# Moving the small Newton steps from GpSimd to VectorE in a fused scan and mixture-of-experts kernel, with a new order of the first loads and another way to sum two tiles of experts

## The chip, the cores and the metric

The kernel runs on one core of a Trainium2 chip. A core has five engines, each of which carries out its own instructions in the order in which they stand in its stream: TensorE (PE; its weight loads are listed apart as PEld), VectorE (DVE), ScalarE (ACT), GpSimd (POOL) and SyncE (SP). SP only issues DMA transfers here; POOL issues some too. The engines wait for each other by semaphores. PE writes into PSUM, the other memory is SBUF, and all tensors start and end in DRAM. The metric is the device time of one execution in microseconds (us).

## The reference, cut to what matters

The input `x` has 8 batches of 1024 rows of 256 values, in float32. One block of a network is computed: a layer norm with a shift and a scale per batch, a selective state-space scan, a residual, a second layer norm, a mixture of 8 experts of which each row takes the best two, and a second residual.

```python
h = _layernorm(x, axis=-1) * (1 + ca) + sa
x = x + ga * attn(h)
h = _layernorm(x, axis=-1) * (1 + cb) + sb
x = x + gb * ffn(h)
# attn: 16 states n for each of the 256 channels d
dt = softplus(dt_raw @ W_dt.T + b_dt);  A = -exp(A_log)
state[l] = exp(dt * A[n]) * state[l-1] + dt * h * B[n]     # a scan over the 1024 rows
y = sum_n state * C[n] + h * D
# ffn: probs = softmax(h @ Wg); the gates of the two best, summing to 1
out = sum over the two best e of gate[e] * (h @ We[e] + be[e])
```

The vectors `sa, ca, ga, sb, cb, gb` come from `silu(c) @ wmod`, one set per batch.

## The kernel before, in words

**Stages.** The rows are cut into 16 stages of 512 rows, two per batch; a stage has four tiles of 128 rows. Channels lie on the 128 partitions in two halves (`j` = 0, 1), so a tensor of one stage is 128x1024. Stages are numbered from 0 here; stage 14 is the last but one.

**The scan part** (`state`, L1001) runs over the 16 states `n`. For each, POOL makes `v` = `du` times the row of B that a DMA has spread over all partitions (L1029, one 128x1024 instruction), ACT makes `a` = exp(dt A) (L1040, two), and DVE scans (L1051, two). Then the scan's result is multiplied by the row of C: by DVE in two 128x512 instructions into `hcD` (L1065), or by POOL in one 128x1024 instruction in place in `hs` (L1070). Which of the two does it is written in `C_ENG`, a letter D or P for each `n`: one string for stages 0 and 1, one for the first halves of batches (stages 2, 4 ... 12), one for the second halves (3, 5 ... 13), one for stages 14 and 15. PE adds the 16 products up in PSUM while it transposes them (L1122). ACT keeps the last column for the next stage (L1057, L1061).

**The norms** (`statistics` L781, `factors` L799). DVE takes mean and variance of each tile (L786, L789); ACT makes a first guess of 1/sqrt(variance + eps) (L808 to L811); and one Newton step improves it, five instructions on 128x8 values, `newton` (L813), each of which needs the one before it. They are POOL's. The first norm of stage s+2 and the second norm of stage s share one Newton step, so there are 14 of this size (back parts of stages 0 to 13), two for the first norms of stages 0 and 1, one for stage 14 and two for stage 15.

**The experts** (`back`, L1149). The normed rows are split in a high and a low part; PE makes the logits; seventeen small instructions of DVE and ACT pick the two best ("route"). The gates go, as a high part by ACT (L1297) and a low part by POOL (`gates_lo`, L1299), through PE to the sum of the biases. For each tile and each pair of experts PE makes six matmuls into one PSUM bank (`expert_pair`, L1336). In stages 0 to 14 ACT weighs the two results by the gates (L1418), and PE adds them up by four transposing matmuls (L1428); a sum of two tiles is scaled by `gb` on ACT (L1435), turned back by PE (L1443), copied by ACT (L1449), and POOL's DMA adds it in DRAM to the `x` that SP has stored there (L1501). In stage 15 (`finish`, L1349) DVE adds each expert's result times its gate to an accumulator in SBUF (L1363), multiplies by `gb` (L1370), adds `x` (L1374), and SP stores the tile.

**What sets the order.** When the program is built, every operation is handed to a planner (`Plan`, L230) with an engine, an assumed cost, the data that it needs, the buffers that it takes, and a due time from the table `DUE` (L35), one number or one per phase (stage 0, stage 1, stages 2 to 13, stage 14, stage 15). `emit` (L304) plays the engines through in assumed time; whenever an engine is free it takes, among the operations that could start within that engine's `PATIENCE`, the one with the lowest due time. The order found so is written out as the fixed order of each engine's stream, DMA queues included. On the chip nothing is reordered: an instruction that waits holds up all behind it on its engine. The first loads are in `setup` (L518): on SP's queue c, wmod, x of stages 0 and 1, W_x, W_dt, be; on POOL's the four small ones D, A, Wg, b_dt. DVE also does the small setup work there (`clamp`, L642: four instructions on 128x16 values, twice).

Of the kernel before, what the change touches and what calls it, by code (L numbers as in the profile page):

```python
# [13 lines left out]
ALU = mybir.AluOpType  # L14
# [15 lines left out]
C_ENG = ("DDPDDPDDPDDPDDPD", "DPDDPDPDPDPDPDDD", "DPDPDPDPDPDPDPDD", "DDPDDPDDPDDPDDDD")  # L30
AHEAD = 1668.1
PATIENCE = {"ACT": 0.14, "DVE": 0.13, "PE": 0.25, "POOL": 0.5, "SP": 0.28}
# [5 lines left out]
    "load c": -2243.51,  # L38
    "load wmod0": -2004.07,
    "load wmod1": -1988.48,  # L40
    "load wmod2": -2.06,
    "load wmod3": -1957.81,
    "load W_x": -1.71,
    "load W_dt": -1965.24,
    "load b_dt": -116.61,
    "load A": -369.4,
    "load D": -1656.1,
    "load Wg": -357.62,
    "Wg hi": -1640.08,
    "Wg lo": -1616.04,  # L50
    "c^T": -414.35,
    "exp c": -1984.89,
    "1 + exp c": -351.35,
    "1 / c": -1644.2,
    "silu c": -1648.48,
    "mod1": -29.89,
    "mod1 out": -1640.92,
    "mod1 + 1": -57.77,
    "mod2": -97.07,
    "mod2 out": -2072.57,  # L60
    "mod3": -2117.64,
    "mod3 out": -1963.21,
    "mod3 + 1": -1953.8,
    "ga0": -437.02,
    "ga1": -460.54,
    "ga2": -73.86,
    "ga3": -2623.36,
    "gb0": -1953.35,
    "gb1": -357.52,
    "gb2": -461.1,  # L70
    "gb3": -27.31,
    "ga mod": -63.28,
    "ga mod D": 262.7,
    "1 / ga": -76.35,
    "gb^T": 279.89,
    "gb out": -406.31,
    "gb store": -483.98,
    "W_x^T": -3768.39,
    "W_x out": -436.84,
    "W_dt^T": -374.71,  # L80
    "W_dt out": -436.11,
    "exp A": -369.97,
    "-A": -74.32,
    "be rows": -2072.64,
    "be hi": -98.66,
    "be lo": -1963.34,
    "be": -55.72,
    "eps": -4332.43,
    "gates hi": (-235.79, -2460.72, -339.79, -149.99, -1797.16),
    "gates lo": (-24.1, -2044.84, -2133.06, -343.23, -3860.41),  # L90
    "load be": -15.49,
    "iw": -70.2,
    "load x": (-1989.96, -1978.86, -17.48, 8.4, -7.21),
    "stats1": (-2009.67, -1972.63, -69.27, -86.05, 47.99),
    "aggr1": (-1640.3, -1975.3, -1.3, -91.31, -2296.04),
    "before1": (-107.3, 986.06, -2961.9, -2961.25, -2977.69),
    "rstd1": (-359.36, 14.85, -2578.96, -2707.53, -2572.88),
    "norm1": (-24.76, -3800.78, 53.71, -15.89, -19.88),
    "trans1_0": (-2098.37, 28.07, -3664.64, -2478.96, -2711.13),
    "modg_0": (962.12, -427.57, -16.09, -2517.23, -444.87),  # L100
    "modD_0": (-1969.85, -43.93, -15.26, 0.47, -464.06),
    "trans1_1": (-2098.96, -16.51, -1646.42, -70.34, -17.88),
    "modg_1": (962.68, 28.65, -3869.23, -4.95, -390.32),
    "modD_1": (-16.02, -141.37, -3869.42, -2640.81, -526.1),
    "W_x / ga": (-2440.92, -1341.87, -50.77, -365.17, -1339.66),
    "proj": (-46.32, -3262.07, -1417.18, -7075.25, -1106.5),
    "rows": (-113.21, 892.07, -2147.14, -25.83, -373.01),
    "spill": (-1509.92, -46.65, -82.13, -108.28, -408.55),
    "dt0": (-2836.1, -86.93, -410.11, -472.19, -22.27),
    "softplus0": (8.96, -483.31, -563.94, -2696.95, -430.27),  # L110
    "dt1": (-2436.14, 985.9, -367.41, -1987.69, -75.38),
    "softplus1": (-3763.28, -2241.26, -2842.46, -2274.94, -367.03),
    "du": (-486.18, -2239.99, -70.63, -2154.13, -1629.08),
    "load B": (-1369.55, -17.6, -22.69, -296.42, -29.81),
    "load C": (-0.98, -16.67, 9.77, -2484.98, -15.04),
    "v": (-499.25, -85.1, -76.35, -47.8, 21.22),
    "a0": (-416.33, -341.56, -12.06, -392.16, -398.23),
    "a1": (-2633.56, -2630.9, -2268.36, -376.87, -2271.91),
    "scan0": (-345.29, -130, -84.13, -483.71, 835.51),
    "keep0": (-2622.16, -2801.29, -2480.02, -431.11, -2842.99),  # L120
    "C0": (-421.59, -408.48, -2258.73, -2296.35, -21.24),
    "scan1": (-350.22, -136.94, -86.02, -2760.06, -4.38),
    "keep1": (-2229.92, -335.27, -2547.2, -437.52, -439.8),
    "C1": (-414.5, -73.48, -2299.69, -2313.25, -19.25),
    "C": (-493.68, -127.22, -2167.24, -2223.87, 18.97),
    "y D": (19.24, -476.83, -54.5, -465.41, -8.25),
    "y": (-2254.19, -1637.88, -9.88, -1109.95, -3.56),
    "y C": (-473.82, -1635.95, -9.36, -7.82, 0.38),
    "load We": 4.3,
    "We hi": 992.95,  # L130
    "We lo": -499.19,
    "x + y": (-2642.38, -4495.38, -2303.57, -15.13, 893),
    "store x": (-2250.83, -2697.53, -2498.03, -14.55, -4714.94),
    "stats2": (-456.02, -1616.02, -2198.38, 0.86, -442.22),
    "aggr2": (-1761.59, -1623.66, -1485.56, 4.02, -32.11),
    "before2": (-53.78, -586.98, -7.88, 277.95, -2145.97),
    "rstd2": (-1659.97, -76.28, -71.01, -1965.28, -301.08),
    "norm2": (-15.76, -2440.99, -2156.75, 21.3, -62.97),
    "trans2_0": (-427.62, -2364.93, -1608.28, -17.84, 261.41),
    "hi0": (-2629.72, -4055.61, -4630.1, -3019.49, -2113.5),  # L140
    "mod2_0": (-343.91, -1615.01, -2238.87, -947.94, -35.03),
    "lo0": (-1317.6, -80.15, -2289.65, -464.16, 16.03),
    "trans2_1": (-3111.61, -1780.04, -10.03, -2604.76, 261.39),
    "hi1": (-2600.7, -738.55, -2256.02, 51.68, -2142.05),
    "mod2_1": (-359.16, -1823.24, -2242.34, -2256.16, 65.08),
    "lo1": (-2347.63, -3887.63, -77.67, -574.96, -1738.61),
    "logits^T": (-86.05, 0.71, -4.18, 0.12, 26.21),
    "logits out": (-2084.24, -89.2, -2470.09, -2118.52, -71.72),
    "logits": (-589.23, -70.63, -1938.4, -18.59, -408.58),
    "route": (-2625.88, -2360.01, -3907.92, -64.39, -2292.96),  # L150
    "gates": (-133.28, -75.36, -3858.04, -2448.11, -2203.07),
    "gates^T": (-2898.97, -1962.73, -2234.43, -4003.16, 6.19),
    "gates out": (-85.21, -9.58, -616.13, -18.22, -363.26),
    "biases": (-1642.72, -1.18, 6.14, 4.55, -932.33),
    "expert0": (-1632.13, -334.88, 2.48, 0.74, 28.86),
    "weigh0": (-2623.2, -2251.01, -2465.87, -2251.67, -3291.15),
    "sum0": (-1630.65, -2.35, 6.77, 2.59, 343.88),
    "gb": (-6.16, -2002.75, -2252.74, -1770.24, -2231.99),
    "turn": (13.97, 2.84, 5.77, -17.42, 288.49),
    "out": (-2240.75, -63.84, -406.3, -1777.56, -2456.12),  # L160
    "expert1": (-89.29, -20.09, 1.79, 275.85, 64.81),
    "weigh1": (-5.26, -122.87, -2272.08, -2165.17, -179.06),
    "sum1": (-5.22, -8.29, 3.93, 280.73, -101.5),
    "store": (-32.73, -46.88, -15.77, 11.83, -2124.92),
    "load gb": (-1904.24, -1904.24, -1904.24, -1904.24, -2839.22),
    "last bias": -92.62,
    "last": -2205.05,
    "last expert": 307.58,
    "last store": -16.76,
# [252 lines left out]
def kernel(  # L422
# [23 lines left out]
    nc = tc.nc  # L446
# [71 lines left out]
    def setup():  # L518
# [6 lines left out]
        def add(kind, eng, cost, fn, r=(), w=(), use=(), psm=None, xfer=0.0, duty=1.0, table=None):  # L525
            ring = [(rings[k], k) for k in use] + ([("psm", psm)] if psm else [])
            cold = 2.0 if duty == 1.0 else 1.3
            plan.add(
                kind, eng, cost, 0.0, fn, r=r, w=w, ring=ring, xfer=xfer, duty=duty, cold=cold, table=table
            )  # L530

        def load(kind, xfer, out_, in_, w, use=(), eng="SP"):
            q = nc.sync if eng == "SP" else nc.gpsimd
            add(
                kind, eng, 0.475 if eng == "SP" else 0.95, lambda: q.dma_start(out=out_(), in_=in_), w=[w],
                use=use, xfer=xfer,
            )
# [97 lines left out]
        add("mod1", "PE", 2.8, lambda: mod_mm(0, 2, pm), r=[sc_k, wm_k[0]], w=[pm], psm=pm, duty=0.05)  # L635
        add("mod1 out", "DVE", 0.15, lambda: mod_out(0, 2, pm), r=[pm], w=[m01])
        add("mod1 + 1", "DVE", 0.07, lambda: plus1(1), w=[m01])
        add("mod2", "PE", 1.4, lambda: mod_mm(2, 3, pg), r=[sc_k, wm_k[1]], w=[pg], psm=pg, duty=0.05)
        add("mod2 out", "DVE", 0.09, lambda: mod_out(2, 3, pg), r=[pg], w=[m2])

        ts, stt = nc.vector.tensor_scalar, nc.vector.scalar_tensor_tensor
# [921 lines left out]
```

## Time and profile before

| | us |
|---|---|
| median of 3 runs | 1039.54 (1039.06 to 1041.3) |
| the profiled execution, its own time | 1040.26 |
| its span, first to last instruction | 1038.5 |
| busy: DVE, PE, POOL, ACT | 959.8, 928.7, 918.5, 845.7 |
| first scan starts, last scan ends | 34.67, 988.66 |

The span is 1.8 us shorter than the execution's own time; the rest lies around it. Busy time counts an engine's instructions as they overlap in time; matmuls are pipelined, so a busy PE need not be at its peak. In a timeline line the columns are start, duration, engine, line of the kernel, operation, output and inputs with shapes and count, and in brackets the idle time before it and what ended that. In a group's line the numbers behind the bar are busy us, mean ns of one, and idle us before. In a table of windows each row has the stretch, its length, and the busy us of each engine with the number of instructions.

From the starts of the scans the stages can be told apart: the 32 scans of stage 2 begin at 154.9, those of stage 13 at 800.2, of stage 14 at 861.6, of stage 15 at 925.3. In between a stage takes 58.5 to 59.5 us from stage 5 to stage 12.

### The profile page before, as it was taken

Reading aid. Unit: us, or ns where it says so; the run is one execution under the profiler, and the core shown is the slowest. Engines: PE = TensorE matmul, PEld = TensorE weight load, DVE = VectorE, ACT = ScalarE, POOL = GpSimd, SP = SyncE. Lnnn points to the kernel's source line nnn. Section 1 sums busy time; section 2 is a strip of 40 time slices with the busy share of each in tenths; the row PEclk is TensorE's granted clock in tenths of the full one; section 3 lists DMA queues with packets and bytes.
Section 4 is the critical chain, followed back from the end, with each engine's and each line's share of the span. In section 5 each row is a group of like instructions: output and inputs, shape, how many; then the busy total and the mean of one; then the engine's idle time right before and its main releaser. Section 6 shows DMA issues by size and latency. Waiting matters only on the chain. (4 is left out here: it accounts for less than half of the span.)

```text
span 1038.5 us, 17114 instructions
## 1 busy us (share of the span) xinstructions
PE 928.7 (89%) x5525; PEld 739.9 (71%) x5525; DVE 959.8 (92%) x1488; ACT 845.7 (81%) x1845; POOL 918.5 (88%) x515
## 2 busy tenths in 40 slices
PE   6656798798899989999999989999998998999998
PEld 4444676586676868687777868688686867778886
DVE  3798999999999999999999999999999998999947
ACT  5855678889699988988899988988898986988661
POOL 4999879999999999999999999999999997988600
PEclk9657998899899999999999999999999999999999
DMA  6556327375655647475665737475575637656102
GB/s 203 185 182 219 122 88 234 96 209 147 194 157 156 208 108 211 113 217 155 166 221 146 219 85 212 123 209 175 138 240 128 221 67 204 169 148 198 39 6 46
DMA packets 103865, 165.20 MB, mean 159 GB/s; under 512 B 10160, under 2 KB 37216, under 8 KB 103776
## 3 DMA queue, kind: packets, MB, share of 16 engines
q1 hardware_dynamic: 95728, 156.22, 49.4%
q0 software_dynamic: 8048, 7.89, 5.1%
q8 instruction: 44, 0.72, 0.3%
q14 instruction: 45, 0.37, 0.1%
HBM read 146.76 MB, written 17.31 MB: 158 GB/s over the span
## 5 line engine op out<-in xcount | busy, mean ns | idle before, releaser
L1029 POOL TENSOR_TENSOR v<-du,bb 128x1024 f32<-128x1024 f32 x255 | 605.8, 2404 | 17.8 <-DMA bb<-bcd 11.7
L1040 ACT ACTIVATE a<-dt,negA 128x512 f32<-128x512 f32 x512 | 348.5, 697 | 52.9 <-DVE hcD L1065 33.0
L1070 POOL TENSOR_TENSOR hs<-hs,cc 128x1024 f32<-128x1024 f32 x96 | 229.9, 2396 | 17.1 <-issue 8.7
L1065 DVE TENSOR_TENSOR hcD<-a,cc 128x512 f32<-128x512 f32 x320 | 214.2, 684 | 13.9 <-ACT carry L1057 7.0
L1418 ACT ACTIVATE wt<-pe,G 128x256 f32<-128x256 f32 x480 | 201.6, 474 | 18.5 <-PE pe L1340 16.8
L1122 PE MATMUL y<-ident,hcD 128*128 128x128 f32 x1280 | 183.3, 285 | 34.8 <-DVE hcD L1065 34.6
L1051 DVE TENSOR_TENSOR_SCAN a<-a,v 128x512 f32<-128x512 f32 x166 | 195.6, 1213 | 8.5 <-POOL v L1029 4.8
L1051 DVE TENSOR_TENSOR_SCAN a<-a,carry,v 128x512 f32<-128x512 f32 x154 | 196.2, 1277 | 1.4 <-POOL v L1029 0.7
L1122 PEld LDWEIGHTS y<-ident,hcD 128*128 128x128 f32 x1280 | 153.8, 147 | 58.0 <-DVE hcD L1065 44.2
L1340 PE MATMUL pe<-we_hi,hi 128*128 128x512 f32 x512 | 179.2, 431 | 7.3 <-ACT wt L1418 4.3
L1340 PE MATMUL pe<-we_lo,hi 128*128 128x512 f32 x512 | 160.7, 395 | 0.0
L1340 PE MATMUL pe<-we_hi,lo 128*128 128x512 f32 x512 | 160.5, 395 | 0.0
L1428 PE MATMUL ma<-ident,wt 128*128 128x128 f32 x960 | 135.8, 275 | 1.2 <-ACT wt L1418 1.2
L1122 PE MATMUL y<-ident,hs 128*128 128x128 f32 x768 | 109.7, 285 | 24.2 <-POOL hs L1070 23.9
L1051 DVE TENSOR_TENSOR_SCAN hs<-a,carry,v 128x512 f32<-128x512 f32 x102 | 125.2, 1266 | 0.0
L1428 PEld LDWEIGHTS ma<-ident,wt 128*128 128x128 f32 x960 | 112.1, 141 | 16.2 <-ACT wt L1418 2.0
L1122 PEld LDWEIGHTS y<-ident,hs 128*128 128x128 f32 x768 | 92.1, 146 | 37.4 <-POOL hs L1070 31.1
L1340 PEld LDWEIGHTS pe<-we_lo,hi 128*128 128x128 f32 x512 | 96.3, 188 | 22.9
L1340 PEld LDWEIGHTS pe<-we_hi,lo 128*128 128x128 f32 x512 | 96.1, 188 | 23.1
L1051 DVE TENSOR_TENSOR_SCAN hs<-a,v 128x512 f32<-128x512 f32 x90 | 106.3, 1208 | 0.0
L1340 PEld LDWEIGHTS pe<-we_hi,hi 128*128 128x128 f32 x512 | 81.5, 190 | 25.6 <-ACT wt L1418 9.2
L831 ACT ACTIVATE xn<-x,ln 128x256 f32<-128x256 f32 x128 | 72.0, 599 | 3.0 <-POOL ln L820 3.0
(134 smaller groups left out, 936.9 us busy)
## 6 DMA issues: line engine op xcount, KB each, us to landing
bb<-bcd SPq DMA_DIRECT2D x256, 256.0 KB, 5.5
cc<-bcd SPq DMA_DIRECT2D x256, 256.0 KB, 5.2
x<-in_L_attn_u_dram SPq DMA_DIRECT2D x16, 512.0 KB, 3.7
out_dram<-x SPq DMA_DIRECT2D x15, 512.0 KB, 3.4
out_dram<-of POOLq DMA_DIRECT2D x15, 512.0 KB, 12.1
wf<-in_L_ffn_We_dram SPq DMA_DIRECT2D x8, 256.0 KB, 4.1
wm<-in_L_wmod_dram SPq DMA_DIRECT2D x2, 512.0 KB
bcd<-xd SPq DMA_DIRECT2D x32, 32.0 KB, 1.6
```

What stands on the lines that cost most here:

```text
L831: nc.scalar.activation(new("xn", xn, [P, TG, D])[:, k, :], T[x][:, k0 + k, :], AF.Identity, bias=T[ln][:, 1, o + k : o + k + 1], scale=T[l ...
L1029: nc.gpsimd.tensor_tensor(new("v", v, [P, DC, CL])[:, :, :cl], T["du", s][:, :, :cl], both(T[bb][:, :cl]), ALU.mult,)
L1040: nc.scalar.activation(new("a", a + (j,), [P, CL])[:, :cl], T["dt", s][:, j, :cl], AF.Exp, scale=negA[:, j, n : n + 1],)
L1051: nc.vector.tensor_tensor_scan(part(j), T[a + (j,)][:, :cl], T[v][:, j, :cl], init, ALU.mult, ALU.add)
L1065: nc.vector.tensor_tensor(new("hcD", hc, [P, DC, CL])[:, j, :cl], part(j), T[cc][:, :cl], ALU.mult)
L1070: nc.gpsimd.tensor_tensor(o, o, both(T[cc][:, :cl]), ALU.mult)
L1122: nc.tensor.matmul(new("y", y, [P, 2, D])[:, k % 2, j * P : (j + 1) * P], T[src][:, j, k * P : (k + 1) * P], ident, is_transpose=True, sta ...
L1340: nc.tensor.matmul(pe, T[v][:, j, k * P : (k + 1) * P], w[:, j, 2 * q : 2 * q + 2, :].rearrange("p e d -> p (e d)"), start=n == 0, stop=n ...
L1418: nc.scalar.activation(new("wt", wt, [P, 2, D])[:, i, :], T["pe", s, part, q, k][:, i * D : (i + 1) * D], AF.Copy, scale=T[G][:, k, e : e ...
L1428: nc.tensor.matmul(o[:, j, (k % 2) * P : (k % 2 + 1) * P], T["wt", s, q, k][:, i, j * P : (j + 1) * P], ident, is_transpose=True, start=Fa ...
```

## The change

Three things are named, and the whole plan is searched anew around them.

1. The Newton step's five instructions and the low part of the gates become VectorE's. The string of `C_ENG` for stages 2, 4 ... 12 goes from six P to seven.
2. The due times of the first loads change: on SP's queue x of stage 0 comes first, then be, c, wmod (first part), W_dt, x of stage 1, wmod (second and fourth part), We, W_x; on POOL's queue the order becomes b_dt, D, Wg, A, and the planner assumes that POOL's small loads share the DMA engines with less weight (`pkt` 0.02 in place of 0.1), so that it counts on their landing later.
3. In stage 14 the tiles 2 and 3 are treated like those of stage 15: bias, eight weighted additions per tile by DVE, times `gb`, plus `x`, and one store per tile by SP. The stores of `x` and POOL's adding store of that stage cover tiles 0 and 1 alone, and `gb` is loaded once, for stage 14.

Besides, all of `DUE` and some assumed costs are new (they change only the order), and three orderings within PE's own stream are written as dependencies.

```diff
-C_ENG = ("DDPDDPDDPDDPDDPD", "DPDDPDPDPDPDPDDD", "DPDPDPDPDPDPDPDD", "DDPDDPDDPDDPDDDD")
-AHEAD = 1668.1
-PATIENCE = {"ACT": 0.14, "DVE": 0.13, "PE": 0.25, "POOL": 0.5, "SP": 0.28}
+C_ENG = ("DDPDDPDDPDDPDDPD", "DPDPDPDPDPDPDPDD", "DPDPDPDPDPDPDPDD", "DDPDDPDDPDDPDDDD")
+AHEAD = 1833.68
+PATIENCE = {"ACT": 0.14, "DVE": 0.22, "PE": 0.23, "POOL": 0.51, "SP": 0.18}
...
-    "load x": (-1989.96, -1978.86, -17.48, 8.4, -7.21),
+    "load x": (-4389.52, -120.89, -66.7, 11.15, 0.38),
...
-    "load c": -2243.51,
-    "load wmod0": -2004.07,
+    "load c": -2337.1,
+    "load wmod0": -122.63,
...
-                kind, eng, 0.475 if eng == "SP" else 0.95, lambda: q.dma_start(out=out_(), in_=in_), w=[w],
-                use=use, xfer=xfer,
+                kind, eng, 0.475 if eng == "SP" else 0.8, lambda: q.dma_start(out=out_(), in_=in_), w=[w],
+                use=use, xfer=xfer, pkt=0.1 if eng == "SP" else 0.02,
...
-            r, m, v, tt = row(0), row(1), row(2), nc.gpsimd.tensor_tensor
+            r, m, v, tt = row(0), row(1), row(2), nc.vector.tensor_tensor
             tt(m, r, r, ALU.mult)
             tt(m, m, v, ALU.mult)
-            nc.gpsimd.tensor_scalar(m, m, -0.5, 1.5, ALU.mult, ALU.add)
+            nc.vector.tensor_scalar(m, m, -0.5, 1.5, ALU.mult, ALU.add)
             tt(r, r, m, ALU.mult)
             tt(m, row(3), r, ALU.mult)
...
-        plan.add("rstd" + n_, "POOL", 0.95 + 0.055 * n, t, newton, r=[st], w=[ln])
+        plan.add("rstd" + n_, "DVE", 0.4, t, newton, r=[st], w=[ln])
...
+        ts_ = tg if s < len(stages) - 2 else 2
+
         def store_x():
-            nc.sync.dma_start(out=orow, in_=T[x][:, k0 : k0 + tg])
+            nc.sync.dma_start(out=orow[:, :ts_], in_=T[x][:, k0 : k0 + ts_])
...
-            nc.gpsimd.tensor_tensor(
+            nc.vector.tensor_tensor(
                 T[gs][:, :tg, 1], T[G][:, :tg], T[gs][:, :tg, 0].bitcast(F32), ALU.subtract
             )
...
-        plan.add("gates lo", "POOL", 0.22, t, gates_lo, r=[G, gs + (0,)], w=[gs + (1,)], ring=("gs", gs))
+        plan.add("gates lo", "DVE", 0.1, t, gates_lo, r=[G, gs + (0,)], w=[gs + (1,)], ring=("gs", gs))
...
-        if last:
-            gb = ("gb", b)
+        half = s == len(stages) - 2
+        turns = [] if last else [("lgd", s)] + ([("ex", s - 1)] if s else [])
+        gb = ("gb", b)
+        if half:
...
-        def finish():
-
-            acc = ("of", s, part)
+        def finish(tiles, acc, name):
...
         if last:
-            finish()
+            finish(range(tg), ("of", s, part), "last")
             return
...
+            if half and p:
+                finish(tiles, of, "half")
+                continue
```

## The prediction

> **What bounds the kernel now.** I read the page first, for busy time and its course, then windows by stage, then who waits for whom, then the timeline where small DVE instructions stand beside POOL's. Of the page, the 40 slices:
>
> ```profile
> DVE  3798999999999999999999999999999998999947
> POOL 4999879999999999999999999999999997988600
> ```
>
> Both are full from the third slice on; POOL falls empty in the last two, DVE does not. The windows, cut where the scans of stages 2, 14 and 15 begin and where the last scan ends:
>
> ```profile
> core 0: us, PE busy (x) PEld busy (x) DVE busy (x) ACT busy (x) POOL busy (x), PEclk, DMA share, GB/s
> ...
> 154.90:800.20 645.30, 595.36 (x3655) 476.00 (x3654) 628.23 (x939) 567.51 (x1243) 628.35 (x334) 0.98 0.59 170
> ...
> 861.60:925.30 63.70, 59.81 (x372) 47.53 (x371) 57.43 (x87) 54.64 (x132) 54.73 (x30) 1.00 0.63 170
> 925.30:988.70 63.40, 62.96 (x404) 53.33 (x403) 61.54 (x86) 49.50 (x107) 47.10 (x27) 1.00 0.42 116
> 988.70:1038.50 49.80, 44.77 (x230) 35.16 (x228) 28.70 (x85) 19.28 (x56) 3.71 (x13) 0.97 0.12 25
> ```
>
> In stages 2 to 12 DVE and POOL are each busy 97% of 645.3 us and idle 17 us. From 925 to the end PE is full and DVE has room. What DVE waits for in stages 2 to 12:
>
> ```profile
> DVE hcD L1065 <- ACT carry L1057: 4.4, 17, 0.5
> DVE a L1051 <- POOL v L1029: 1.7, 8, 0.5
> DVE a L1051 <- ACT a L1040: 1.6, 4, 0.4
> ```
>
> Only 7.7 us are waits for others; the rest of the 17 lies between instructions that need each other. So DVE can take up hardly any work unseen. What a small DVE instruction costs beside POOL, at three moments (DVE and POOL rows put together):
>
> ```profile
> 14.72 0.14 DVE L653 TENSOR_SCALAR tmp<-modT 128x16 f32<-128x16 f32 x1
> ...
> 32.00 1.27 POOL L968 TENSOR_TENSOR du<-dt,g 128x512 f32<-128x512 f32 x1
> 32.02 1.28 DVE L653 TENSOR_SCALAR tmp<-modT 128x16 f32<-128x16 f32 x1
> 33.35 1.28 POOL L1035 TENSOR_TENSOR v<-du,bb 128x512 f32<-128x512 f32 x1
> 33.42 1.25 DVE L655 SCALAR_TENSOR_TENSOR tmp<-modT 128x16 f32<-128x16 f32 x1
> ...
> 47.36 2.37 POOL L1070 TENSOR_TENSOR hs<-hs,cc 128x1024 f32<-128x1024 f32 x1
> 48.94 0.83 DVE L656 SCALAR_TENSOR_TENSOR modT<-tmp 128x16 f32<-128x16 f32 x1
> ```
>
> The same TENSOR_SCALAR takes 0.14 us when POOL rests and 1.28 when POOL began just before it. All three slow ones end within 0.04 us of the end of POOL's instruction (33.27, 34.63, 49.73): they wait for it. Large two-input instructions do not:
>
> ```profile
> L1029 POOL TENSOR_TENSOR v<-du,bb 128x1024 f32<-128x1024 f32 x255 | 605.8, 2404 | 17.8 <-DMA bb<-bcd 11.7 <-DVE a L1051 2.9 <-issue 1.2
> L1065 DVE TENSOR_TENSOR hcD<-a,cc 128x512 f32<-128x512 f32 x320 | 214.2, 684 | 13.9 <-ACT carry L1057 7.0
> ```
>
> 295 of the 320 `hcD` began while POOL was at work, and none took more than 0.694.
>
> **The change, part by part**, against the profiled execution's 1040.26.
>
> *Newton, on POOL.* One step holds POOL from 282.8 to the next `v`:
>
> ```profile
> 278.06 4.74 POOL L1029 TENSOR_TENSOR v<-du,bb 128x1024 f32<-128x1024 f32 x2
> 282.74 0.21 POOL L816 TENSOR_TENSOR ln<-ln 128x8 f32<-128x8 f32 x1
> ...
> 284.05 2.40 POOL L1029 TENSOR_TENSOR v<-du,bb 128x1024 f32<-128x1024 f32 x1
> ```
>
> That is 1.27 us; `gates_lo` (0.287) about 0.33 with its gap: 14 x 1.6 = 22.4 off POOL. One more `C` in each of six stages puts 6 x 2.35 = 14.1 back. POOL ends 8.3 lighter; it is not the bound, so this is worth nothing itself.
>
> *Newton, on DVE.* Five instructions in a chain. Small chained DVE instructions (routing) start 0.21 to 0.23 apart, and one with nothing chained behind it gives way after 0.11: 4 x 0.21 + 0.11 = 0.95, and 14 x 0.95 = +13.3. The other five Newton steps lie at the start or in the tail, where DVE has room. `gates_lo`: 14 x 0.11 = +1.5. The six moved `C` take two `hcD` each off DVE, which start 0.60 apart: 12 x 0.60 = -7.2.
>
> *The wait for POOL.* The third of the five is a TENSOR_SCALAR from SBUF to SBUF, like L653. The trace has none in the middle stages, so I bound it: 0 if it finds POOL between instructions each time, 2.4 if POOL has always just begun. POOL is busy 97% with instructions of 2.4 us, and nothing in the plan ties the two, so I take half a `v`: 0.97 x 1.2 = 1.17, 14 x 1.17 = +16.4 (ends 0 and +33.6). Behind it on DVE's stream stand the scans; ACT's `a` buffers and PE's sums wait for those.
>
> The Trainium skill, page "SBUF — State Buffer", section "Who interferes with whom", speaks against this change: VectorE and GpSimd share a port pair, `tensor_scalar` can take both ports, and the second to issue blocks until the first is done. L653 agrees (0.14 against 1.28). The page also has a VectorE instruction with two SBUF inputs contend with a GpSimd read; `hcD` at 684 ns disagrees. By the page each of the five would wait for a POOL instruction and the sum would be that of the third rival below; by the rows only one does, and the sum is the one given here; the measurement decides.
>
> *What DVE's waits give back.* DVE later and POOL lighter: the waits for `v` and `a` (1.7 + 1.6) go, and I count half of the 4.4 behind ACT's carry: -5.5. In stage 14 DVE idles 6.3 us (63.70 less 57.43), which hides one stage's addition (0.95 + 0.11 + 1.17): -2.2.
>
> *The start.* DVE's stream is held until 9.76 by the small loads: `-A` runs at 8.90 after 4.8 us of waiting for ACT and POOL's load of A, `Wg lo` at 9.67, and only then come the statistics of `x`. With `x` first (issue to landing 3.7 in the page's row) these could begin near 4.5. But wmod's first part moves from SP's second place to the sixth, four issues of 0.4 to 0.5 later, so `mod1` starts near 6.6, not 5.09: 3.56 for `mod1`, 1.88 for `mod2`, about 1.5 for the clamps and what follows them (14.72 to 16.3 now), so the products `gd` could start at 13.5 in place of 17.48. Best end -3.9. Worst: A is now POOL's last load, and if the plan counts on it too early it holds DVE 1.8 longer: +1.8. I take -2.0, nearer the gain, since wmod's own chain is the surer row. SP's remaining loads only change places.
>
> *The tail.* Tiles 2 and 3 of stage 14 lose 8 sums of four matmuls that start 0.109 apart (3.5) and one turn (0.44); biases change one for one. PE is full from 925 on, so -3.9; least 0, if DVE's work sets the end instead. DVE gets 16 additions at 0.52 and four of 0.43, 10 us, where it is busy 28.7 of 49.8. ACT loses 16 x 0.474 there and idles anyway. SP issues two small stores more and one `gb` load fewer, beside PE.
>
> *The new order* of everything else I take at 0: the waits above bound its gain at about 2, and the plan's assumed 0.4 for a step that takes 0.95 + 1.17 can lose as much.
>
> Sum: 13.3 + 1.5 - 7.2 + 16.4 - 5.5 - 2.2 - 2.0 - 3.9 = +10.4: 1050.7. The median of the runs lies 0.7 below the profiled time, so 1050.0.
>
> **The rivals.** *No wait for POOL, so faster.* Everything else stays: 10.4 - 16.4 = -6.0, or 1033.6. For it: four slow cases at most in one trace, all on 128x16 values, none in the middle stages; and a step can fall where POOL waits for a DMA. Against it: the same operation, type and memory, and a POOL that rests 3% of the time. It decides when the mean wait per step falls under 1.17 - 10.4 / 14 = 0.43 us.
>
> *The gains at both ends don't come.* The small load holds DVE (+3.8 against my sum) and PE's tail is not shorter because DVE's 10 us get in its way (+3.9): 1057.7. For it: in the tail DVE follows PE within 0.5 us. Against it: both have idle time beside them.
>
> *All five wait.* L655 and L656 have two SBUF inputs and waited. If small size, not the operation, made them wait, a step costs up to five POOL instructions, 12 us: 14 x 10.9 more, about 1200. Against it: `hcD`, and L654, which slipped in at 33.33 between two POOL instructions.
>
> **How the numbers follow.** A change under 0.2% (2.1 us) can't be told from none. Forecast 0.55, with its own range 1043 to 1058; no wait 0.32; no gains at the ends 0.09; all five 0.04. The 8 in 10 reach from 1030, under the second case with the best start, to 1058. Slower: 0.55 + 0.09 + 0.04, less 0.04 for the forecast's low end, where `same` lies: 0.64. Faster 0.32, same 0.04.
>
> **What would show it.** Right: the TENSOR_SCALAR of the Newton step on DVE spreads from 0.15 to 2.4 with a mean above 1, and ends when a POOL instruction ends; the four TENSOR_TENSOR of it stay at 0.2; a stage takes about 60 us, DVE idle less, POOL more; the first scan starts near 32.7; PE's `ma` matmuls are 32 fewer. Wrong: a TENSOR_SCALAR at 0.2 throughout; or a pace of 59 us with the waits there; or a tail from the last scan to the end other than 46.

## The result, and the profile after

| | before | after |
|---|---|---|
| median of four runs of each, us | 1040.42 (1039.06 to 1041.84) | 1130.98 (1129.76 to 1140.25) |
| the profiled execution: its own time, its span | 1040.26, 1038.5 | 1131.07, 1129.3 |
| busy DVE, PE, POOL, ACT | 959.8, 928.7, 918.5, 845.7 | 1061.4, 954.7, 911.2, 842.9 |
| stages 2 to 12 (first scan of stage 2 to first scan of stage 13) | 645.3 | 720.6 |

The change made the kernel slower: after is 1.089 times before, with a 95% interval of 1.083 to 1.095 (the two medians alone give 1.087). The prediction was 1050.0 with a range of 1030 to 1058; the sign was right, and the size was not: about 90 us were lost in place of about 10.

First the 40 slices of the page of after, two rows of them:

```profile
DVE  4799999999999999999999999999999999999988
POOL 4887998988899977888898889989898888767700
```

DVE is as full as before, but over a longer span: 102 us more busy time in all. POOL, which was full too, now has gaps (eights and sevens). So DVE, busy for 94% of the span, is now the one full engine, and what has to be found is what it does in 102 us more. The windows of after, cut at the first scans of stages 2, 13, 14 and 15 and at the end of the last scan (columns: stretch, its length, busy us of PE, PEld, DVE, ACT and POOL with the number of instructions, clock, DMA share, GB/s):

```profile
155.80:876.40 720.60, 630.62 (x3740) 510.53 (x3739) 697.05 (x1003) 579.31 (x1260) 631.14 (x275) 0.94 0.52 152
876.40:944.00 67.60, 62.19 (x379) 50.40 (x378) 64.34 (x94) 54.42 (x110) 57.49 (x26) 0.97 0.51 151
944.00:1014.70 70.70, 64.83 (x379) 50.83 (x378) 66.47 (x99) 56.99 (x137) 52.53 (x23) 0.95 0.45 138
1014.70:1080.40 65.70, 60.78 (x376) 50.58 (x376) 63.91 (x80) 44.86 (x95) 45.66 (x21) 0.97 0.45 119
1080.40:1129.30 48.90, 41.81 (x195) 31.16 (x193) 39.31 (x117) 13.35 (x40) 1.21 (x1) 0.97 0.09 22
```

75 of the 91 us come in stages 2 to 12, where DVE is busy 697 us in place of 628; the tail is even shorter (48.9, before 49.8). Which instructions take the time is in the groups of after, each shape by itself (line, engine, operation, output and inputs, count; behind the bar busy us, mean ns of one, idle us before):

```profile
L1070 DVE TENSOR_TENSOR hcD<-a,cc 128x512 f32<-128x512 f32 x308 | 205.7, 683 | 10.8 <-ACT carry L1062 5.7 <-issue 0.2
...
L1309 DVE TENSOR_TENSOR gs<-G,gs 128x32 fp32r<-128x32 f32 x15 | 32.5, 2165 | 0.0
...
L820 DVE TENSOR_TENSOR ln<-ln 128x8 f32<-128x8 f32 x14 | 15.9, 1134 | 0.0
L821 DVE TENSOR_TENSOR ln<-ln 128x8 f32<-128x8 f32 x14 | 15.1, 1081 | 0.7
...
L822 DVE TENSOR_SCALAR ln<-ln 128x8 f32<-128x8 f32 x14 | 8.7, 623 | 0.5
L823 DVE TENSOR_TENSOR ln<-ln 128x8 f32<-128x8 f32 x14 | 8.5, 611 | 0.5
L824 DVE TENSOR_TENSOR ln<-ln 128x8 f32<-128x8 f32 x14 | 6.5, 466 | 0.7
```

The large `hcD` keep their 683 ns. The instructions that the change gave to DVE do not keep theirs: the low part of the gates holds DVE for 2165 ns, the five of the Newton step for 466 to 1134. All six kinds together, 112 instructions of every shape, hold DVE for 100.1 us. The same ones take 0.14 to 0.17 where POOL has nothing in flight, so about 19 us would be their own time (112 x 0.165 = 18.5), and some 81 us are added. Two stretches of the timeline of after show with what. DVE's row first (start, duration, engine, line):

```profile
363.90 0.69 DVE L1070 TENSOR_TENSOR hcD<-a,cc 128x512 f32<-128x512 f32 x1
364.51 0.36 DVE L820 TENSOR_TENSOR ln<-ln 128x8 f32<-128x8 f32 x1
364.90 2.30 DVE L821 TENSOR_TENSOR ln<-ln 128x8 f32<-128x8 f32 x1
367.24 2.28 DVE L822 TENSOR_SCALAR ln<-ln 128x8 f32<-128x8 f32 x1
369.55 0.17 DVE L823 TENSOR_TENSOR ln<-ln 128x8 f32<-128x8 f32 x1
369.75 0.17 DVE L824 TENSOR_TENSOR ln<-ln 128x8 f32<-128x8 f32 x1
...
594.03 5.00 DVE L1309 TENSOR_TENSOR gs<-G,gs 128x32 fp32r<-128x32 f32 x1
```

and POOL's in the same two stretches:

```profile
362.43 4.75 POOL L1034 TENSOR_TENSOR v<-du,bb 128x1024 f32<-128x1024 f32 x2 [0.87 <-DMA bb<-bcd]
367.13 2.36 POOL L1075 TENSOR_TENSOR hs<-hs,cc 128x1024 f32<-128x1024 f32 x1
...
593.91 2.77 POOL L1075 TENSOR_TENSOR hs<-hs,cc 128x1024 f32<-128x1024 f32 x1
596.21 2.76 POOL L1034 TENSOR_TENSOR v<-du,bb 128x1024 f32<-128x1024 f32 x1
```

L820 ends at 364.87, between two `v`. L821 ends at 367.20, where the second `v` does (367.18). L822 ends at 369.52, where `hs` does (369.49). Then POOL has nothing to do, and L823 and L824 take 0.17 each. The gates' low part ends at 599.03 with the second of two POOL instructions (598.97): it sat through the rest of one and the whole of the next. It isn't the TENSOR_SCALAR alone that waits, as the prediction had it. Every one of the six does.

Who waits behind them is in the list of waits of after: ACT with the normed rows `xn`, PE with the gates in `pl`, POOL with its next `v` (waiting engine and line, the one waited for, total us, times, longest):

```profile
ACT xn L835 <- DVE ln L824: 56.0, 17, 6.1
...
PE pl L1315 <- DVE gs L1309: 43.2, 12, 5.6
...
POOL v L1034 <- DVE a L1056: 23.6, 14, 2.7
```

The third of these was 2.9 us in 3 times before: while DVE stands, no scan sets a `v` buffer free, and POOL runs out of them. That fits what the chains of five show: none of the 19 waits more than three times (3 of them three times, 7 twice, 5 once, 4 never).

### The profile page after: what moved, and what is told of

The parts are those of the page before. It is cut to its first block, busy times and chain, and to the rows that moved or that the text cites. A ratio compares the mean times of both kernels' runs of the same rounds, so it can differ in the third digit from the quotient of the medians.

```text
span 1129.3 us, 16974 instructions
## 1 busy us (share of the span) xinstructions
PE 954.7 (85%) x5489; PEld 764.3 (68%) x5489; DVE 1061.4 (94%) x1608; ACT 842.9 (75%) x1824; POOL 911.2 (81%) x409
## 5 line engine op out<-in xcount | busy, mean ns | idle before, releaser
L1034 POOL TENSOR_TENSOR v<-du,bb 128x1024 f32<-128x1024 f32 x255 | 617.5, 2468 | 86.0 <-DVE a L1056 23.6
L1075 POOL TENSOR_TENSOR hs<-hs,cc 128x1024 f32<-128x1024 f32 x102 | 251.8, 2469 | 33.6 <-ACT carry L1066 11.3
L1430 ACT ACTIVATE wt<-pe,G 128x256 f32<-128x256 f32 x464 | 194.2, 469 | 30.5 <-PE pe L1353 22.5
L1070 DVE TENSOR_TENSOR hcD<-a,cc 128x512 f32<-128x512 f32 x308 | 205.7, 683 | 10.8 <-ACT carry L1062 5.7
L1056 DVE TENSOR_TENSOR_SCAN a<-a,v 128x512 f32<-128x512 f32 x154 | 182.7, 1211 | 16.9 <-POOL v L1040 12.2
L1353 PE MATMUL pe<-we_hi,hi 128*128 128x512 f32 x512 | 186.6, 447 | 4.1 <-ACT wt L1430 1.7
L1353 PE MATMUL pe<-we_lo,hi 128*128 128x512 f32 x512 | 165.7, 406 | 0.0
L1127 PE MATMUL y<-ident,hs 128*128 128x128 f32 x816 | 115.5, 283 | 14.9 <-POOL hs L1075 14.9
L1056 DVE TENSOR_TENSOR_SCAN hs<-a,v 128x512 f32<-128x512 f32 x102 | 121.7, 1207 | 2.3 <-ACT a L1045 2.2
L1127 PEld LDWEIGHTS y<-ident,hs 128*128 128x128 f32 x816 | 98.7, 147 | 27.9 <-POOL hs L1075 18.3
```

Source lines behind the costliest of these rows:

```text
L1034: nc.gpsimd.tensor_tensor(new("v", v, [P, DC, CL])[:, :, :cl], T["du", s][:, :, :cl], both(T[bb][:, :cl]), ALU.mult,)
L1056: nc.vector.tensor_tensor_scan(part(j), T[a + (j,)][:, :cl], T[v][:, j, :cl], init, ALU.mult, ALU.add)
L1070: nc.vector.tensor_tensor(new("hcD", hc, [P, DC, CL])[:, j, :cl], part(j), T[cc][:, :cl], ALU.mult)
L1075: nc.gpsimd.tensor_tensor(o, o, both(T[cc][:, :cl]), ALU.mult)
L1127: nc.tensor.matmul(new("y", y, [P, 2, D])[:, k % 2, j * P : (j + 1) * P], T[src][:, j, k * P : (k + 1) * P], ident, is_transpose=True, sta ...
L1353: nc.tensor.matmul(pe, T[v][:, j, k * P : (k + 1) * P], w[:, j, 2 * q : 2 * q + 2, :].rearrange("p e d -> p (e d)"), start=n == 0, stop=n ...
```

## The experiments

The theory from these rows: each of the six instructions waits for POOL's instruction in flight, since it reads two tensors from SBUF (or is a TENSOR_SCALAR from SBUF, like the slow L653 of before), and `hcD` and the scans don't, since `a` lies in PSUM. The rivals: only short instructions wait, whatever they read; or the new order of everything else costs the time.

### Parts undone or done alone, with a new plan

Three kernels undid or did a part and let the planner make a new order. In `both_back` Newton's step and the low part of the gates go back to POOL in the kernel after:

```diff
-            r, m, v, tt = row(0), row(1), row(2), nc.vector.tensor_tensor
+            r, m, v, tt = row(0), row(1), row(2), nc.gpsimd.tensor_tensor
...
-        plan.add("rstd" + n_, "DVE", 0.4, t, newton, r=[st], w=[ln])
+        plan.add("rstd" + n_, "POOL", 0.95 + 0.055 * n, t, newton, r=[st], w=[ln])
...
-        plan.add("gates lo", "DVE", 0.1, t, gates_lo, r=[G, gs + (0,)], w=[gs + (1,)], ring=("gs", gs))
+        plan.add("gates lo", "POOL", 0.22, t, gates_lo, r=[G, gs + (0,)], w=[gs + (1,)], ring=("gs", gs))
```

> The changed kernel with the Newton step and the gates' low part on POOL again; all else of the change stays. Theory 1 (the small VectorE instructions wait for POOL): they hold DVE for 100.1 us where 112 of them at 0.17 would take 19, so 81 us go, and about 15 us of DVE work with them: 1030 to 1045, level with the kernel before. Theory 2 (the seventh P, the half stage and the new order cost it): still above 1100.

In `gates_back` the gates' low part alone goes back:

> The changed kernel with only the gates' low part on POOL again. Theory 1: its 17 instructions hold DVE 32.8 us in the changed kernel, 30 more than unhindered, so 1095 to 1105, and the Newton instructions wait as before. Theory 2: within 5 us of 1131.

In `newton_alone` the Newton step goes to DVE in the kernel before, with the due times of `rstd1` and `rstd2` from the kernel after, since with the old ones the planner finds no order (besides the lines shown, `newton` is issued by `nc.vector`, as in the diff of the change):

```diff
...
-        plan.add("rstd" + n_, "POOL", 0.95 + 0.055 * n, t, newton, r=[st], w=[ln])
+        plan.add("rstd" + n_, "DVE", 0.4, t, newton, r=[st], w=[ln])
```

> The kernel before with the Newton step alone on VectorE (its two due times are the changed kernel's, since the planner finds no order with the old ones). Theory 1: the waits of the Newton instructions (67.3 us held, 16 if unhindered) and 14 us of work come on top: 1085 to 1110, and the TENSOR_TENSOR of the step take up to 2.4 us like the TENSOR_SCALAR. Theory 2: at most 1050.

All three missed. `both_back` took 1114.91 us (ratio to before 1.0725, 95% 1.0703 to 1.0748), `gates_back` 1173.96 and `newton_alone` 1188.31 in one run each. In `both_back` the six instructions are POOL's again and none of them holds DVE, and yet it is 74 us slower than before. Its list of waits shows engines that wait for each other in turn:

```profile
DVE a L1056 <- POOL v L1034: 33.3, 9, 14.0
POOL ln L820 <- ACT ln L813: 31.3, 9, 13.5
```

The due times of the table were found for one set of engines and costs; with one step on another engine they give an order that nobody chose. So these three runs don't give the price of a part, for or against either theory. From here on the order was held fixed.

### The step without the second SBUF input, in the order of after

`no_port` keeps after's order instruction for instruction. The five instructions and the low part of the gates become as many TENSOR_REDUCE over an axis of one, of the same shapes, each of which reads one SBUF tensor. That leaves out the refinement, the scaling of the mean and the gates' subtraction.

```diff
-            tt(m, r, r, ALU.mult)
-            tt(m, m, v, ALU.mult)
-            nc.vector.tensor_scalar(m, m, -0.5, 1.5, ALU.mult, ALU.add)
-            tt(r, r, m, ALU.mult)
-            tt(m, row(3), r, ALU.mult)
+            def one(o, i):
+                nc.vector.tensor_reduce(o, i.unsqueeze(2), AX.X, ALU.max)
+
+            one(m, r)
+            one(m, v)
+            one(m, m)
+            one(r, r)
+            one(m, row(3))
...
-            nc.vector.tensor_tensor(
-                T[gs][:, :tg, 1], T[G][:, :tg], T[gs][:, :tg, 0].bitcast(F32), ALU.subtract
-            )
+            nc.vector.tensor_reduce(T[gs][:, :tg, 1], T[G][:, :tg].unsqueeze(3), AX.X, ALU.max)
```

> The changed kernel with every engine's order as it is; only the five instructions of each Newton step and the gates' low part are replaced by TENSOR_REDUCE over an axis of one, of the same shapes on the same tiles, which read one SBUF tensor through one port. Left out by that: the refinement, the scaling of the mean, the subtraction. Theory 1 (the wait for the port, now with the order held fixed): the 81 us of waits go from DVE, which is the bound, and 1035 to 1055 is left. Theory 2 (the rest of the change, or its order): above 1100.

It took 1043.27 us (1041.88 to 1046.72), 1.0023 times before (1.0007 to 1.0038). With the same number of instructions on DVE, in the same place, 1130.98 - 1043.27 = 87.7 of the 90.6 us are gone. The windows of `no_port`, cut at the same events as those of after:

```profile
149.30:803.60 654.30, 613.83 (x3747) 488.04 (x3746) 633.57 (x1004) 579.72 (x1263) 629.64 (x275) 0.99 0.58 168
803.60:866.10 62.50, 60.51 (x373) 48.08 (x372) 59.78 (x93) 53.89 (x107) 57.80 (x26) 1.00 0.59 151
866.10:931.90 65.80, 62.86 (x378) 50.19 (x377) 60.78 (x100) 56.98 (x136) 52.53 (x23) 0.97 0.52 149
931.90:991.65 59.75, 58.90 (x375) 49.14 (x375) 58.09 (x80) 44.72 (x95) 45.62 (x21) 1.00 0.51 132
991.65:1040.50 48.85, 41.61 (x195) 31.21 (x193) 39.02 (x117) 13.35 (x40) 1.21 (x1) 0.99 0.09 22
```

Stages 2 to 12 have almost the same number of DVE instructions as in after (1004, 1003), and DVE is busy 633.6 in place of 697.1. The stand-ins take no more than the instructions of after do where POOL rests, beside a POOL that is busy for 629.6 of the 654.3 us:

```profile
L821 DVE TENSOR_REDUCE ln<-ln 128x8 f32<-128x8 f32 x70 | 9.5, 158 | 1.3
...
L1312 DVE TENSOR_REDUCE gs<-G 128x32 fp32r<-128x32 f32 x15 | 2.5, 169 | 0.0
```

This settles how much of the loss hangs on what these instructions read, not yet by which of the two properties, two inputs or the kind of operation.

`no_port_gates` replaces only the low part of the gates, the last hunk of the diff above:

> The changed kernel in its own order; only the gates' low part is replaced by a TENSOR_REDUCE over an axis of one (the subtraction is left out), the Newton step stays. Theory 1: of the 32.8 us that these 17 instructions hold DVE, 30 go: 1095 to 1105. Less, if POOL runs ahead in its waits and the Newton steps then meet a busier POOL: up to 1120.

It took 1107.87 us in one run, a little more than the first range expected. So in this order taking the wait from the gates' low part alone is worth 1130.98 - 1107.87 = 23.1 us, and taking it from the Newton step after that 1107.87 - 1043.27 = 64.6. What they hold DVE for too long in after is 30.0 (32.9 for 17 instructions, less 17 x 0.17) and 51.5 (67.2 for 95, less 95 x 0.165). The two prices differ from these since the two waits depend on each other. Two groups of `no_port_gates`, whose lines in after were 15.9, 1134 and 15.1, 1081:

```profile
L820 DVE TENSOR_TENSOR ln<-ln 128x8 f32<-128x8 f32 x14 | 20.2, 1442 | 0.0
L821 DVE TENSOR_TENSOR ln<-ln 128x8 f32<-128x8 f32 x14 | 17.2, 1230 | 0.7
```

With the gates' wait gone, the 95 instructions of the Newton steps hold DVE for 75.8 us in place of 67.2: 32 of them last over 0.3 us, in after 28. So 30.0 us go and 8.6 come back, which is 21.4 of the 23.1; and 60.1 (75.8 less 95 x 0.165) is then left for the Newton step, of the 64.6. What remains of each is a few us, and the four runs of after alone spread over 10.

### The same six in the order of before

`before_order_dve` is the kernel before with its own order; only the issuing engine of the six is another, at the places where POOL had them:

```diff
-            r, m, v, tt = row(0), row(1), row(2), nc.gpsimd.tensor_tensor
+            r, m, v, tt = row(0), row(1), row(2), nc.vector.tensor_tensor
...
-            nc.gpsimd.tensor_scalar(m, m, -0.5, 1.5, ALU.mult, ALU.add)
+            nc.vector.tensor_scalar(m, m, -0.5, 1.5, ALU.mult, ALU.add)
...
-            nc.gpsimd.tensor_tensor(
+            nc.vector.tensor_tensor(
```

> The kernel before in its own order, but the Newton step and the gates' low part are issued on VectorE at the place where they stand; the planner still counts them on POOL. Theory 1: the waits come with them, 80 us and 15 us of work: 1110 to 1150. Theory 2: at most 1060.

One run took 1120.40. The old order loses about 80 us by the same edit, without the moved loads, the moved `C` or the additions of stage 14. With `no_port`, where the new order without the wait is level with before, that rules out the rival that the new order costs the time.

`order_kept_pool` is the opposite: the order of after, the six issued by POOL at their places.

> The changed kernel with the order that the planner found for it, but the Newton step and the gates' low part are issued on POOL, at the place in the order where they stand. Nothing else moves, unlike both_back, where the planner ordered everything anew. Theory 1: the waits go and POOL gets 22 us of work that it has idle time for: 1040 to 1065. Theory 2: above 1100. If both_back's 1115 came from the new order alone, this run is well below it.

It took 1084.56 us, 1.042 times before (1.038 to 1.0459), above what was expected. Its waits point to the reason:

```profile
DVE a L1056 <- ACT a L1045: 27.7, 25, 3.8
...
POOL ln L820 <- ACT ln L813: 27.0, 4, 15.0
...
POOL gs L1309 <- ACT gs L1306: 12.5, 2, 8.4
```

POOL meets these instructions before ACT has made their inputs, waits for up to 15.0 us, and holds up its own `v` behind them. The order of after was made for a POOL without these steps. That these waits make up the whole of the loss is not shown. So putting the step back wins 46 us of the 90 in this order and not all; the order before and the step on POOL belong together.

### What waits, measured by itself

`beside_pool` leaves the reference's computation out. It runs groups of DVE instructions first with POOL at rest and then beside 150 of POOL's 128x1024 multiplications.

```diff
+    groups(6)
+    nc.vector.tensor_copy(bb[:, 512:], o)
+    for i in range(150):
+        nc.gpsimd.tensor_tensor(vs[i % 2], du, bb, ALU.mult)
+    groups(12)
```

> The disputed cost by itself; the computation of the reference is left out, the input is copied to the output. Groups of VectorE instructions run first with POOL at rest and then beside 150 of POOL's 128x1024 products. If shortness makes an instruction wait: TENSOR_TENSOR of 8 and 32 values wait 1 to 2.4 us, those of 512 and the scans keep 0.69 and 1.2, and somewhere between lies an edge. If the operation makes it: TENSOR_SCALAR and SCALAR_TENSOR_TENSOR wait at every size, TENSOR_TENSOR at none. If two SBUF inputs make it, as the skill's page on SBUF has it: every size waits but the product with one input in PSUM.

Its groups in the first stretch, POOL at rest (`r` and `o` lie in SBUF, `pm` in PSUM):

```profile
L54 DVE TENSOR_TENSOR_SCAN o<-r,r 128x512 f32<-128x512 f32 x6 | 7.3, 1224 | 0.2
...
L44 DVE TENSOR_TENSOR o<-r,r 128x512 f32<-128x512 f32 x6 | 4.2, 693 | 0.2
...
L48 DVE TENSOR_SCALAR o<-r 128x8 f32<-128x8 f32 x6 | 1.0, 172 | 0.2
L46 DVE TENSOR_TENSOR o<-pm,r 128x8 f32<-128x8 f32 x6 | 1.0, 166 | 0.2
...
L36 DVE TENSOR_TENSOR o<-r,r 128x8 f32<-128x8 f32 x6 | 0.9, 156 | 0.2
```

and in the second, beside POOL:

```profile
L54 DVE TENSOR_TENSOR_SCAN o<-r,r 128x512 f32<-128x512 f32 x12 | 38.2, 3186 | 0.4
L44 DVE TENSOR_TENSOR o<-r,r 128x512 f32<-128x512 f32 x12 | 32.5, 2711 | 0.4
...
L48 DVE TENSOR_SCALAR o<-r 128x8 f32<-128x8 f32 x12 | 27.0, 2247 | 0.4
...
L36 DVE TENSOR_TENSOR o<-r,r 128x8 f32<-128x8 f32 x12 | 25.0, 2082 | 0.4
L46 DVE TENSOR_TENSOR o<-pm,r 128x8 f32<-128x8 f32 x12 | 2.0, 166 | 0.4
```

Size decides nothing here. A 128x8 product and a 128x512 product from SBUF each lose about 2 us, as do a scan, a scalar_tensor_tensor (425 to 2444) and a TENSOR_SCALAR. One product loses nothing, 166 to 166: the one with an input in PSUM. The Trainium skill, page "SBUF — State Buffer", section "Who interferes with whom", states exactly that a VectorE instruction with two SBUF inputs contends with a GpSimd instruction that reads SBUF, and that one with at most one SBUF input, outside the two-port modes, does not. These rows agree with both halves.

### The other way round: the scan's `a` in SBUF

If that is the rule, the kernel before is fast because `a` lies in PSUM, and moving it must be ruinous. `a_in_sbuf` is the kernel before in its own order with one buffer moved:

```diff
-    "of": 2,
+    "of": 2, "as": 3,
...
-                new("a", a + (j,), [P, CL])[:, :cl], T["dt", s][:, j, :cl], AF.Exp,
+                new("as", a + (j,), [P, CL])[:, :cl], T["dt", s][:, j, :cl], AF.Exp,
```

> The kernel before in its own order; the three buffers of the decay a lie in SBUF and no longer in PSUM, so that the scans and the products hcD read two SBUF tensors. If two SBUF inputs make a VectorE instruction wait for POOL (theory 1 as the bare measurement has it), every one of 512 scans and 320 products now waits for up to one POOL instruction, and DVE and POOL take turns: the 832 instructions end on POOL's 360 or so only in part, so 1500 to 2300. If only short instructions wait (my reading in the prediction, that the products wait for nothing since they are large), 1035 to 1060.

One run took 1728.34 us, beside 1039.12 for the kernel before. Groups of `a_in_sbuf`:

```profile
L1029 POOL TENSOR_TENSOR v<-du,bb 128x1024 f32<-128x1024 f32 x255 | 751.2, 2962 | 70.6 <-DVE a L1051 41.7 <-issue 13.6 <-PE y L1122 6.5
L1065 DVE TENSOR_TENSOR hcD<-a,cc 128x512 f32<-128x512 f32 x320 | 554.7, 1748 | 9.3 <-PE y L1122 1.2 <-issue 0.9
...
L1051 DVE TENSOR_TENSOR_SCAN a<-a,v 128x512 f32<-128x512 f32 x166 | 338.5, 2068 | 4.4 <-ACT a L1040 4.0 <-issue 0.4
```

The same 320 `hcD` that never took more than 0.694 us beside POOL now take 1748 ns in the mean. It isn't SBUF as such: with POOL at rest `beside_pool` has 693 ns for such a product, beside the 684 of `hcD` with `a` in PSUM. The rival "short instructions only" falls, and with it the argument on which the prediction had rejected the page's rule. POOL's instructions grow too, from 2404 to 2962 ns.

## Why the prediction was wrong

**The step that failed** is the reading of the `hcD` rows under "What a small DVE instruction costs beside POOL": "Large two-input instructions do not" wait. The rows are right; what they were taken for is wrong. `hcD<-a,cc` has one input in SBUF, since `new` puts the ring `a` into the PSUM pool `ps_a`, and the same goes for the scans. So the `hcD` that ran undisturbed beside POOL said nothing on instructions with two SBUF inputs; with such inputs a product of this size takes 2711 ns beside POOL (`beside_pool`) and 693 without it. From that reading the page's rule was set aside, the four TENSOR_TENSOR of the step and the gates' low part were costed at their bare time, with no wait, and the true case became the third rival with a chance of 0.04. What the runs showed in its place: all six kinds of instruction wait, and the wait is worth 87.7 us in place of 16.4.

The trace of before could have told it. These are some of DVE's groups in its stages 2 to 12, which the prediction did not use:

```profile
L1194 DVE TENSOR_TENSOR lo<-pt,hi 128x512 fp32r<-128x512 f32 x22 | 14.7, 672 | 0.0
L1158 DVE TENSOR_TENSOR x<-x,y 128x512 f32<-128x512 f32 x20 | 12.6, 674 | 0.0
...
L1251 DVE TENSOR_TENSOR pl<-pl,rt 128x32 f32<-128x32 f32 x11 | 2.2, 199 | 0.4
...
L1261 DVE TENSOR_TENSOR rt<-pl,rt 128x32 f32<-128x32 f32 x11 | 2.1, 191 | 0.4
...
L1271 DVE TENSOR_TENSOR G<-pl,rt 128x32 f32<-128x32 f32 x11 | 2.1, 190 | 0.3
```

All of them run beside a POOL that is 97% busy and none is slow; and every one has a PSUM tensor among its inputs (`pt`, `y`, `pl`). No row in these stages has two SBUF tensors as inputs; the slow L655 and L656 of the start were such rows. "The trace has none in the middle stages" was the right sentence, but for all six instructions and not for the TENSOR_SCALAR alone.

**The terms of the sum, one by one.**

*The wait for POOL*, +16.4 for the TENSOR_SCALAR alone: measured 87.7, as the difference of after and `no_port`. The TENSOR_SCALAR itself waits less than taken: 0.623 - 0.17 = 0.45 in the mean, not 1.17: in 16 of the 19 steps POOL had nothing in flight when it began, in 11 of these after one or two waits of the instructions before it. The four that were costed at nothing wait 0.97, 0.91, 0.44 and 0.30 (their means less 0.165), and the gates' low part 2.0. A whole step waits 3.1, and one stage with its gates 5.1.

*Newton and the gates on DVE without the wait*, +13.3 and +1.5, *and the moved `C`*, -7.2, together +7.6: for stages 2 to 12 alone the same terms make 11 x (0.95 + 0.11) - 7.2 = +4.5, and `no_port`, with its stand-ins, shows DVE busy there 633.6 in place of 628.2, +5.3. Near enough.

*What DVE's waits give back*, -5.5: not seen. From the start to the end of stage 12 DVE is idle for 45.2 us in `no_port` (803.6 less 13.0, 111.8 and 633.6) and was for 45.6 before (800.2 less 12.5, 113.9 and 628.2). DVE's work grows by 3.8 us up to there, and the time by 3.4: work was added to the engine that bounds, and the idle time stayed. That is the sum of two unlike parts: stages 0 and 1 take 115.7 in place of 120.2, and stages 2 to 12 take 654.3 in place of 645.3, of which 5.3 is DVE's work and 3.6 more idle time (20.7, before 17.1).

*The start*, -2.0: `no_port` reaches its first scan 1.0 earlier (33.6, before 34.7), after itself 0.4 later (35.1). In after the statistics of `x` do begin early, at 4.8 in place of 9.8, but `-A` comes at 14.3, where it was 8.9 before, since ACT makes the first norm ahead of it; two of the small setup instructions (L658 and L660) hold DVE for 1.19 and 1.12 us, where POOL is at work; and the products `gd` come at 20.5, not at 13.5. That is nearer the worse of the two ends, and by another way than the late load of A that the prediction had named for it.

*Stage 14's idle time*, -2.2, *and the tail*, -3.9: from the first scan of stage 13 to the end `no_port` takes 236.9 us, before 238.3, so -1.4 for both. PE's `ma` matmuls are 32 fewer as forecast, and PE ends 42.8 after the last scan in place of 44.8; but DVE's weighted additions, a chain 0.52 apart, end 3.0 later still. That is the second rival's mechanism, and near its size: the tail lasts 48.8, where 46 was forecast. What PE gives up shows in stage 15 instead (59.8, before 63.4), and stages 13 and 14 take 3.2 more. The reading that DVE has room from 925 on holds for the tail alone: in stage 15 of before it was busy 61.54 of 63.40 us.

*The order*, 0: not measurable alone. Without the wait the whole change is worth +2.4 us by the ratio of `no_port` (0.23%), where the sum less its wait said -6.0. So even without the wait the time would not have been the 1033.6 of that rival: the gains at both ends and in DVE's waits, which are in the sum in every case, did not come.

**The rivals.** "All five wait" was the right mechanism. Its price, 1200, was too high since it let each of the five wait for a whole POOL instruction; they wait 3.1 us a step instead of 12, and it left out the gates, which wait too.

**The signs named.** Right: the TENSOR_SCALAR spreads from 0.17 to 2.29 and of the 39 of all six kinds that last over 0.3 us, 38 end within 0.06 us of the end of a POOL instruction; DVE idles less (67.9 us, before 78.7) and POOL more; 32 fewer `ma`. Wrong: the mean of the TENSOR_SCALAR is 0.62, not above 1; the four TENSOR_TENSOR do not stay at 0.2 (up to 4.33); a stage takes 65.5 (720.6 / 11), not 60; the first scan starts at 35.1, not 32.7.

## What to carry to other kernels

Before an instruction goes to VectorE beside a busy GpSimd, look up for each input in which memory it lies, in the kernel and not by its name in a row: in these runs, with two inputs from SBUF, or as a TENSOR_SCALAR from SBUF, it waits for GpSimd's instruction in flight, however small it is (156 ns become 2082); with one of two inputs in PSUM it doesn't (166 and 166). Its cost is then the duration of GpSimd's instructions and not its own, so six instructions of 0.17 us could hold VectorE for 5 us more in each stage. And a part of a kernel whose order was searched is priced by changing it inside a fixed order; a new plan around it measures the plan.

## What the runs showed that was not expected

- The one that waits on VectorE may sit through more than the GpSimd instruction in flight: at 594.03 and at 301.00 in after it took 5.00 and 4.33 us, to the end of the next one. In the first case GpSimd's next instruction begins at 596.21, before the one in flight ends (596.68); why it goes ahead of the waiting one is not shown. In `beside_pool` most waits last one GpSimd instruction (2.26 us of a median 2.38), and ten 128x8 products in a row took 20.8 us.
- The wait takes away its own cause: VectorE's stop keeps `v` buffers from coming free, GpSimd runs dry (23.6 us of waits for the scans, before 2.9), and the rest of the chain passes at 0.17 us each.
- One buffer's place, `a` in PSUM, is worth 689 us of 1039 to the kernel before. The Newton step with its inputs in PSUM wasn't tried; the kernel's eight PSUM buffers of 128x512 (rings of 2, 3, 2 and 1) all have another use. An estimate from `no_port`, which has no wait either, is about 1043 for it in the order of after. No version of this change measured here beats the kernel before.
